# Decays of a selective scan: PSUM or SBUF for the units whose products GpSimd makes

## The chip, the core and the metric

The kernel runs on one core of a Trainium2 chip. A core has TensorE (PE, matrix multiplication), VectorE (DVE), ScalarE (ACT, activation functions) and GpSimd (POOL), each with its own instruction queue, and SyncE (SP), which here only issues transfers. Two memories on the core hold 128 partitions each: SBUF, and the smaller PSUM with eight banks, each of which holds 512 fp32 columns. The metric is device time in microseconds (us) for one execution.

## The reference

Four images of 64x64 positions and 128 channels go through four layers. Layer 0 holds the part that matters here, a selective scan in four directions over 4,096 positions, with 256 channels and 16 states for each channel:

```python
def step(h, t):
    x_t, d_t, B_t, C_t = t
    h = jnp.exp(d_t[..., None] * A) * h + (d_t * x_t)[..., None] * B_t[:, :, None, :]
    return (h, jnp.einsum('bkdn,bkn->bkd', h, C_t))
```

The factor `exp(d_t * A)` is the decay. Around the scan layer 0 has a projection, a depthwise 3x3 convolution, normalisations, a gate and an MLP. Layer 1 is attention over all positions of an image, layer 2 a chain of convolutions, layer 3 attention in 7x7 neighbourhoods with an MLP. Everything is fp32.

## The kernel before

**The scan unit.** `selective_scan` treats one image. It walks over the four directions, over eight chunks of 512 positions and over the states. One unit holds 32 channels with 4 states each on the 128 partitions, twice (g = 0, 1), and 512 columns. An image has 512 units, the kernel 2,048. A unit's steps are:

- POOL, L501: `dB` = `du` times a row of B, one instruction of 128x1024 for both g, all in SBUF. `dB` has four buffers.
- ACT, L507: for each g, the decay `dA` = exp(scale x `dt`), 128x512. All units share three PSUM tiles (`bufs=3`), each of one bank.
- DVE, L509: for each g, the scan over 512 columns, from `dA`, `dB` and the state that the chunk before left.
- ACT, L516 or L518: the last column is kept as the next chunk's state.
- The product of the scan's result with a row of C. `ON_POOL` says which engine makes it: in image 0 five, in the later images seven of 16 units have it made by POOL (L522, one instruction for both g). There the scan writes to the SBUF tile `hc`[...]. For the other units the scan writes back over the decay in PSUM and DVE makes the product into `hc` (L514, one instruction for each g).
- PE, L555: sums over the states into the PSUM tile `py`.

A unit is called a P unit below if POOL makes its product and a V unit if DVE does. DVE scans both kinds.

**What runs beside it.** `network` starts with `scan_inputs` for image 0, then scans image after image. Beside the scan of image 0 run `scan_inputs` for the other images; beside the scan of image n (n from 1 to 3) runs `rest` for image n-1, that is the output of its layer 0 (`scan_output`) and its layers 1 to 3; after the last scan, `rest` for image 3. Four of the eight PSUM banks belong to the scan (three for `dA`, one for `py`), the others to what runs beside it until the scan is over.

**Order.** The order on each engine is fixed when the program is built. A scheduler sets it from priorities and from its own idea of durations; the scan has lower priority than the layers beside it. On each engine the instructions then run strictly in that order, each waiting for semaphores of the others. `settle` puts POOL's product two units (`BEHIND`) after the scan that it needs.

**The product buffers.** Once image 0's scan is laid out and the inputs of all images are made, `network` opens an SBUF pool `ss_more` and hands it to `Products.widen`. From then on `products.more` is not None and four further `hc` buffers are in use; the pool lasts until the scan is over.

**Other lines that are named.** L396 and L397 (`softplus`): exp and log of 128x512 on ACT, the first from PSUM to PSUM, the second from PSUM to SBUF. L601 (`scan_output`): DVE adds two 128x128 SBUF tiles, once for each image. L785 (`layer1`): a DVE maximum over 4,096 columns of one SBUF tile. L854 (`layer1`, last image): DVE adds two SBUF tiles of 2,048 columns. L1165 (`layer3_bound`, once): a DVE instruction on one element with two SBUF inputs. L1390 (`layer3_attention`): DVE adds a PSUM tile to an SBUF tile, 512 columns.

Of the kernel before, what the change touches and what calls it, by code (L numbers as in the profile page):

```python
# [28 lines left out]
F32 = mybir.dt.float32  # L29
# [13 lines left out]
LC = 512  # L43
# [24 lines left out]
def mid(ap, n):  # L68

    return bc(ap.unsqueeze(1), [ap.shape[0], n, ap.shape[1]])  # L70
# [383 lines left out]
def selective_scan(tc, K, S, D, img):  # L454
# [9 lines left out]
    pool, psum, products = S.pool, S.psum, S.products  # L464
    waiting = []

    def settle(unit):
        while waiting and waiting[0][0] <= unit:
            waiting.pop(0)[1]()

    for k in ORDER:
# [4 lines left out]
        for i in range(NCH):  # L476
            c = NCH - 1 - i if back else i
            for hf in range(2):
# [11 lines left out]
                for j in range(NJS):  # L490
# [7 lines left out]
                    for pp in range(2):  # L498
                        pr = 2 * hf + pp
                        dB = pool.tile([128, 2, LC], F32, name="dB", bufs=4)  # L500
                        nc.gpsimd.tensor_mul(dB, dus[pp], mid(bt, 2))  # L501
                        on_pool = S.unit % 16 in ON_POOL[img > 0]
                        S.unit += 1
                        hc = products.tile()
                        for g in range(2):
                            dA = psum.tile([128, LC], F32, name="dA", bufs=3)
                            nc.scalar.activation(dA, dts[pp][:, g, :], AF.Exp, scale=S.A[:, k, j, pr, g : g + 1])  # L507
                            hg = hc[:, g, :] if on_pool else dA
                            nc.vector.tensor_tensor_scan(  # L509
                                hg[:, order], dA[:, order], dB[:, g, order],  # L510
                                0.0 if i == 0 else state[:, j, pr, g : g + 1], ALU.mult, ALU.add,
                            )
                            if not on_pool:
                                mm = nc.vector.tensor_mul(hc[:, g, :], dA, ct)  # L514
                                if i < NCH - 1:
                                    nc.scalar.copy(state[:, j, pr, g : g + 1], dA[:, last : last + 1])  # L516
                        if on_pool and i < NCH - 1:
                            nc.scalar.copy(state[:, j, pr, :], hc[:, :, last])  # L518
                        if on_pool:

                            def product(hc=hc, ct=ct, made=made):
                                made.append(nc.gpsimd.tensor_mul(hc, hc, mid(ct, 2)))  # L522

                            waiting.append((S.unit + BEHIND, product))
                        else:
                            made.append(mm)
                        hcs.append(hc)
                        settle(S.unit)
# [1151 lines left out]
def everything_again(tc, K, A, D, out):  # L1680

    K.general = True
    make_shifted_bias(tc, A, D.bias)
    for img in range(B):
        with ExitStack() as ctx:
            S = make_scan(ctx, tc, K, A)
            scan_inputs(tc, K, A, D, img)
            selective_scan(tc, K, S, D, img)
        with ExitStack() as ctx:
            xT = transposed(ctx, tc)  # L1690
            scan_output(tc, K, A, D, img, xT, None)
            layer1(tc, K, A, D, img, xT, False)
            layer2(tc, K, A, D, img, xT, False)
        layer3_shifted(tc, K, A, D, img)
        layer3_mlp_alone(tc, K, A, D, img, out[img], 4)


def network(tc, A, out):
    nc = tc.nc
    with ExitStack() as ctx:  # L1700
# [26 lines left out]
        with ExitStack() as scan_ctx:  # L1727
            S = make_scan(scan_ctx, tc, K, A)
            make_conv_diagonals(tc, K, A, D.conv_diag)
            with priority(tc, K, SCAN_FIRST // 2):  # L1730
                with tc.tile_pool(name="mk_w2", bufs=1, side="right") as pool:
                    make_layer2(tc, K, A, D, pool)
            scan_inputs(tc, K, A, D, 0)
            before = None
            for img in range(B):
                with priority(tc, K, SCAN_FIRST):
                    selective_scan(tc, K, S, D, img)
                if img == 0:
                    make_bias(tc, K, A, D.biasT)
                    for later in range(1, B):  # L1740
                        scan_inputs(tc, K, A, D, later)
                    more = scan_ctx.enter_context(tc.tile_pool(name="ss_more", bufs=1))
                    S.products.widen(more, 4)
                else:
                    rest(tc, K, A, D, img - 1, before)
                    before = img - 1, out[img - 1]
            rest(tc, K, A, D, B - 1, before, scan_ctx.close, out[B - 1])
# [84 lines left out]
```

## Time and profile before

| | |
|---|---|
| median of 3 runs | 8,847.33 us (8,841.02 to 8,850.56) |
| the profiled execution | 8,838.78 us |
| its span, first to last instruction | 8,837.0 us |
| mean TensorE clock granted | 0.860 |
| busy: PE, DVE, ACT, POOL | 7,047.0, 7,137.4, 5,686.9, 7,046.7 us |
| scan of image 0 | 103 to 2,165 us |
| scan of images 1, 2, 3 | 2,165 to 3,983, to 5,815, to 7,637 us |
| after the scan | 7,637 to 8,837 us |

The profile is of one execution. Its page has the busy time of each engine, the span in 40 slices (a digit is the busy share in tenths), the DMA queues, and groups of instructions by line, engine, operation and tile: out<-in, shape and count, then busy us and mean ns of one, then the idle time of the engine before them and what ended most of it. The trace answers further views: sums of each engine's busy time in chosen stretches; waits (engine, line, tile, what it waited for, then total us, times, longest); one line's durations (shortest/median/longest); and a timeline, where a row gives start, length in us, engine, line, operation, tiles and how many instructions of a kind follow each other (x2 means that the length is of both). Idle time of an engine that doesn't set the end costs nothing.

### The profile page before, as it was taken

The page shows a single profiled execution, that of the slowest core. Times are in us where ns is not written, and L with a number is a line of the kernel's source. Part 1 is how long each engine was busy: PE and PEld are TensorE (multiplying, and loading weights), DVE is VectorE, ACT ScalarE, POOL GpSimd, SP SyncE. Part 2 cuts the span into 40 slices and gives each one's busy share as a digit, 9 for nine tenths or more (in the row PEclk, how much of TensorE's full clock was granted, in tenths as well). Part 3 has the DMA queues.
Part 4 walks back from the last instruction along what each step waited for, and adds up shares of the span by engine and source line. Part 5 has one row for each costly group of instructions (what it writes and reads, how often), then busy time and mean ns, then how long its engine had stood idle before and what let it go on. Part 6 is the DMA issues. An engine that isn't in the chain of part 4 may idle for free. (4 is left out here: it accounts for less than half of the span.)

```text
span 8837.0 us, 102218 instructions
## 1 busy us (share of the span) xinstructions
PE 7047.0 (80%) x30532; PEld 2635.0 (30%) x30532; DVE 7137.4 (81%) x8531; ACT 5686.9 (64%) x11661; POOL 7046.7 (80%) x3079
## 2 busy tenths in 40 slices
PE   6745858687788898786788988877789887788988
PEld 2211313132332222333322223333322223344333
DVE  4788978787999999998899999998899999513433
ACT  5646767676676676666766676667766666454366
POOL 6888998989899999997799999998899989500000
PEclk8756869697799998898899998888899998899989
DMA  5777777777554556665455556575455565320020
GB/s 185 244 232 247 241 251 240 260 242 262 189 170 165 170 170 219 191 211 190 160 168 173 174 174 227 194 224 176 156 171 174 176 217 192 108 70 5 1 82 12
DMA packets 855474, 1572.03 MB, mean 178 GB/s; under 512 B 218341, under 2 KB 336764, under 8 KB 851197
## 3 DMA queue, kind: packets, MB, share of 16 engines
q1 hardware_dynamic: 724605, 1389.21, 48.1%
q10 hardware_dynamic: 130304, 176.19, 5.6%
q8 instruction: 245, 4.01, 0.2%
q14 instruction: 320, 2.62, 0.1%
HBM read 1273.92 MB, written 280.18 MB: 176 GB/s over the span
## 5 line engine op out<-in xcount | busy, mean ns | idle before, releaser
L501 POOL TENSOR_TENSOR dB<-du,b_rows 128x1024 f32<-128x1024 f32 x2048 | 4805.9, 2375 | 477.2 <-issue 124.7
L507 ACT ACTIVATE dA<-dt,w_A_log 128x512 f32<-128x512 f32 x4096 | 2781.9, 690 | 510.8 <-DVE hc L509 246.7
L509 DVE TENSOR_TENSOR_SCAN dA<-dA,state,dB 128x512 f32<-128x512 f32 x2128 | 2631.5, 1272 | 275.6 <-POOL dB L501 131.8
L522 POOL TENSOR_TENSOR hc<-hc,c_rows 128x1024 f32<-128x1024 f32 x832 | 1976.6, 2376 | 47.0 <-ACT state L518 21.7
L509 DVE TENSOR_TENSOR_SCAN hc<-dA,state,dB 128x512 f32<-128x512 f32 x1456 | 1801.1, 1267 | 180.5 <-ACT dA L507 105.8
L514 DVE TENSOR_TENSOR hc<-dA,c_rows 128x512 f32<-128x512 f32 x2432 | 1564.5, 675 | 74.4 <-PE py L555 59.3
L555 PE MATMUL py<-hc,pick 128*32 128x512 f32 x8192 | 1245.1, 683 | 392.0 <-POOL hc L522 299.8
L516 ACT COPY state<-dA 128x1 f32<-128x1 f32 x2128 | 326.9, 158 | 1271.7 <-DVE hc L514 1260.1
L845 PE MATMUL pa<-e,l_v 128*128 128x512 f32 x2048 | 1062.5, 651 | 20.3 <-ACT e L801 20.3
L797 PE MATMUL pair<-l_g,l_f 32*128 32x512 f32 x2048 | 532.8, 667 | 165.7 <-ACT e L801 119.1
L801 ACT ACTIVATE e<-pair 128x1024 f32<-128x1024 f32 (+1 forms) x448 | 508.4, 1135 | 231.4 <-PE pair L797 222.8
L985 POOL MEMSET l_h<- 64x128 f32 x8 | 1.6, 197 | 814.9 <-DVE l_h L959 814.9
L845 PEld LDWEIGHTS pa<-e,l_v 128*128 128x128 f32 x2048 | 374.3, 199 | 670.9 <-issue 615.1
L555 PEld LDWEIGHTS py<-hc,pick 128*32 128x32 f32 x8192 | 210.1, 116 | 1161.4 <-issue 471.1
L247 PE MATMUL ps<-band,w_conv_diag 128*128 128x504 f32 (+3 forms) x1152 | 500.4, 594 | 6.0 <-ACT delta L397 6.0
L1351 PE MATMUL pair<-table,ident 128*128 128x512 f32 x768 | 408.2, 657 | 98.7 <-ACT e L1361 76.2
L509 DVE TENSOR_TENSOR_SCAN dA<-dA,dB 128x512 f32<-128x512 f32 x304 | 356.1, 1212 | 66.3 <-POOL dB L501 52.5
L201 PE MATMUL ps<-ident,ln_xn 128*128 128x128 f32 x512 | 141.9, 371 | 325.2 <-ACT ln_xn L198 253.2
L328 POOL TENSOR_TENSOR du<-delta,xc 128x1024 f32<-128x1024 f32 x128 | 333.3, 2611 | 52.6 <-ACT delta L397 46.7
L1361 ACT ACTIVATE e<-pair 128x1024 f32<-128x1024 f32 (+1 forms) x224 | 254.8, 1137 | 178.6 <-PE pair L1355 177.8
L247 PEld LDWEIGHTS ps<-band,w_conv_diag 128*128 128x128 f32 x1152 | 221.3, 193 | 283.9 <-issue 263.8
L797 PEld LDWEIGHTS pair<-l_g,l_f 32*128 32x128 f32 x2048 | 140.6, 189 | 523.9 <-ACT e L801 264.4
(285 smaller groups left out, 8746.8 us busy)
## 6 DMA issues: line engine op xcount, KB each, us to landing
b_rows<-bc_dram SPq DMA_DIRECT2D x1024, 256.0 KB
c_rows<-bc_dram SPq DMA_DIRECT2D x1024, 256.0 KB
dt<-delta_dram SPq DMA_DIRECT2D x512, 512.0 KB
du<-du_dram SPq DMA_DIRECT2D x512, 512.0 KB
delta_dram<-delta ACTq DMA_DIRECT2D x128, 512.0 KB
du_dram<-du SPq DMA_DIRECT2D x128, 512.0 KB
table<-biasT_dram SPq DMA_DIRECT2D x72, 512.0 KB
y_first_dram<-y_sum ACTq DMA_DIRECT2D x128, 256.0 KB
```

What stands on the lines that cost most here:

```text
L247: mm = nc.tensor.matmul(out[:, r0 - row0 : r1 - row0, c0:c1], lhsT((dy + 1) * 3 + dx + 1), src[:, r0 + dy : r1 + dy, c0 + dx : c1 + dx], s ...
L328: nc.gpsimd.tensor_mul(du.rearrange("p d (a b) -> p d a b", b=H), deltas[b].rearrange("p d (a b) -> p d a b", b=H), tk,)
L501: nc.gpsimd.tensor_mul(dB, dus[pp], mid(bt, 2))
L507: nc.scalar.activation(dA, dts[pp][:, g, :], AF.Exp, scale=S.A[:, k, j, pr, g : g + 1])
L509: nc.vector.tensor_tensor_scan(hg[:, order], dA[:, order], dB[:, g, order], 0.0 if i == 0 else state[:, j, pr, g : g + 1], ALU.mult, ALU.add,)
L514: mm = nc.vector.tensor_mul(hc[:, g, :], dA, ct)
L522: made.append(nc.gpsimd.tensor_mul(hc, hc, mid(ct, 2)))
L555: mm = nc.tensor.matmul(py[0][32 * q : 32 * q + 32, :], S.pick, hcs[q // 2][:, q % 2, :], start=(k == 1 and j == 0), stop=(j == NJS - 1),)
L797: nc.tensor.matmul(ps[:, u, :], f[quad, t // 4, span(t % 4, 128)], g[quad, c, :], start=True, stop=True)
L801: made = nc.scalar.activation(e, ps, AF.Exp)
L845: nc.tensor.matmul(pa, v[:, 8 * q + t, :], es[q], start=(t == 0 and q == 0), stop=(t == 7 and q == 3),)
L1351: nc.tensor.matmul(ps[:, u, :], K.ident, t[:, u, :], start=True, stop=False)
```

## The change

Where a unit is a P unit and `products.more` exists, which is so from image 1 on, the decay is a tile of the SBUF pool `ss_more`, named `decays`, with three buffers of 128x512. In all other cases it is the PSUM tile `dA` as before. So in images 1 to 3 the three PSUM tiles hold decays of V units only, and the P units' scans read both the decay and `dB` from SBUF. Instructions, shapes and counts are the same.

```diff
                         hc = products.tile()
                         for g in range(2):
-                            dA = psum.tile([128, LC], F32, name="dA", bufs=3)
+                            if on_pool and products.more is not None:
+                                dA = products.more.tile([128, LC], F32, name="decays", bufs=3)
+                            else:
+                                dA = psum.tile([128, LC], F32, name="dA", bufs=3)
                             nc.scalar.activation(dA, dts[pp][:, g, :], AF.Exp, scale=S.A[:, k, j, pr, g : g + 1])
                             hg = hc[:, g, :] if on_pool else dA
                             nc.vector.tensor_tensor_scan(
```

## The prediction

> **What bounds the kernel now.** I read the 40 slices of the page first, to cut the span into stages; then the sums by stage; then the costliest groups, the waits of VectorE (DVE), and the timelines of DVE and GpSimd (POOL) where a DVE instruction was oddly long.
>
> ```profile
> DVE  4788978787999999998899999998899999513433
> POOL 6888998989899999997799999998899989500000
> ```
>
> Both are at 80 to 100% until slice 35 and POOL then stops: the scan fills nearly all of the span. By the starts of the scan instructions, image 0 is scanned from 103 to 2165 us and images 1 to 3, which alone the edit touches, from 2165 to 7637 us, 5,472 us in all. The sums of these three stages:
>
> ```profile
> core 0: us, PE busy (x) PEld busy (x) DVE busy (x) ACT busy (x) POOL busy (x), PEclk, DMA share, GB/s
> 2165.00:3983.00 1818.00, 1505.29 (x7009) 542.65 (x7012) 1688.75 (x1942) 1197.46 (x2451) 1730.48 (x750) 0.88 0.58 188
> 3983.00:5815.00 1832.00, 1517.16 (x6823) 556.91 (x6818) 1678.62 (x1984) 1242.31 (x2564) 1705.87 (x740) 0.88 0.56 183
> 5815.00:7637.00 1822.00, 1512.80 (x6840) 556.71 (x6839) 1678.85 (x1978) 1240.55 (x2551) 1707.42 (x740) 0.89 0.56 182
> ```
>
> POOL is busy 5,144 of 5,472 us (94%, idle 328), DVE 5,046 (92%, idle 426), ScalarE (ACT) 3,680 (67%). The two lean on each other all the time. The price of each step stands in the groups of the page:
>
> ```profile
> L501 POOL TENSOR_TENSOR dB<-du,b_rows 128x1024 f32<-128x1024 f32 x2048 | 4805.9, 2375 | 477.2 <-issue 124.7
> L507 ACT ACTIVATE dA<-dt,w_A_log 128x512 f32<-128x512 f32 x4096 | 2781.9, 690 | 510.8 <-DVE hc L509 246.7
> L522 POOL TENSOR_TENSOR hc<-hc,c_rows 128x1024 f32<-128x1024 f32 x832 | 1976.6, 2376 | 47.0 <-ACT state L518 21.7
> L509 DVE TENSOR_TENSOR_SCAN hc<-dA,state,dB 128x512 f32<-128x512 f32 x1456 | 1801.1, 1267 | 180.5 <-ACT dA L507 105.8
> L514 DVE TENSOR_TENSOR hc<-dA,c_rows 128x512 f32<-128x512 f32 x2432 | 1564.5, 675 | 74.4 <-PE py L555 59.3
> ```
>
> The scans that write hc are those of GpSimd's units ("P units"), whose product is L522; VectorE's own ("V units") have theirs in L514. What more PSUM tiles could win is in DVE's waits within 2165 to 7637 us:
>
> ```profile
> DVE hc L509 <- ACT dA L507: 96.3, 56, 7.0
> DVE dA L509 <- POOL dB L501: 81.0, 91, 5.1
> DVE dA L509 <- ACT dA L507: 60.6, 41, 4.6
> ```
>
> Waits for a decay come to 157 us. No gain from the added depth can be larger, and behind it stand the waits for dB (122 us with those of the hc scans).
>
> [...] Today each scan reads dA in PSUM and dB in SBUF, one SBUF input, and no scan row shows a block (1,267 ns). After the edit the P units' scans read two. Does the trace know the block? Yes, at L601, an add of two 128x128 SBUF tiles. First DVE's timeline, then POOL's, at that place (start, length):
>
> ```profile
> 2217.06 11.22 DVE L601 TENSOR_TENSOR center<-center,ident 128x128 f32<-128x128 f32 x1
> 2228.20 2.32 DVE L509 TENSOR_TENSOR_SCAN hc<-dA,dB 128x512 f32<-128x512 f32 x2
> ```
>
> ```profile
> 2216.60 6.93 POOL L501 TENSOR_TENSOR dB<-du,b_rows 128x1024 f32<-128x1024 f32 x3
> 2223.50 2.33 POOL L522 TENSOR_TENSOR hc<-hc,c_rows 128x1024 f32<-128x1024 f32 x1
> 2225.79 2.33 POOL L501 TENSOR_TENSOR dB<-du,b_rows 128x1024 f32<-128x1024 f32 x1
> 2230.66 2.44 POOL L501 TENSOR_TENSOR dB<-du,b_rows 128x1024 f32<-128x1024 f32 x1 [2.54 <-DVE hc L509]
> ```
>
> The add takes 0.29 us where POOL is silent (its last occurrence, at 7776 us); here it lasts 11.22 us, through five POOL instructions, and ends 0.16 us after the fifth. Another took 5.60 us, at 5902 us. L1165, a SCALAR_TENSOR_TENSOR of one element with two SBUF inputs, took 5.05 us amid POOL's work, and ended at an edge between two POOL instructions. The control:
>
> ```profile
> L785 DVE TENSOR_REDUCE bounds<-l_v x4: 4412/4420/4420, 2539.4 to 8046.8; 128x1 f32<-128x4096 f32 x4
> ```
>
> A one-input reduction of 4,096 columns has the same length under POOL's work and after it. [...] no row shows a scan with two SBUF inputs, nor POOL held behind DVE.
>
> [...] L854, both inputs in SBUF, takes 2,293 ns for 2,048 columns[...], and L1390, one input in PSUM, 677 ns for 512[...]. I take 0 for it[...]. [...] here L397 (to SBUF) takes 601 ns, L396 (to PSUM) 580.
>
> **The change part by part.** In images 1 to 3, 7 of 16 units are P units: 3 x 512 x 7/16 = 672 units, each with two decays and two scans, so 1,344 of each. No instruction and no DMA is added or removed; in the rebuilt order side work stands 3 to 10 scans later in the mean, 40 at most, of 4,096. I cost that at nothing.
>
> (a) ACT writes 1,344 decays to SBUF: 1,344 x 21 ns = 28 us on an engine idle a third of the time. Nothing on the path; were that cover gone, 28 us.
>
> (b) The three PSUM tiles serve V units alone: a gain of 0 to 157 us, if nothing else came. It can't show while DVE stands longer in (c): 0.
>
> (c) 1,344 scans get a second SBUF input. Two scans of one unit last 2.45 us (timeline of the steady state). While they run, POOL's dB and products, all of which read SBUF, are shut out; while POOL runs, the scans are. So POOL's work and these scans add up: 672 x 2.45 = 1,646 us on top of 5,144 gives 6,790 us if POOL is never idle otherwise, and 7,118 us if it keeps its 328 us of idle time. I take the second, since those gaps come from side work, transfers and full buffers that stay: **+1,646 us**; the low end is 6,790 - 5,472 = +1,318.
>
> Does DVE bear that? A P unit followed by a V unit: POOL has two dB and one product, 7.1 us. DVE has 2.45 (P), then 2.45 + 1.26 (V) and 0.6 of side work, 4.3 us in which POOL may work. 7.1 - 4.3 = 2.8 us of POOL's work falls where DVE stands before its P scans. The pair takes 2.45 + 7.1 = 9.6 us, against 7.1 to 7.3 now. Over the stage: 7,118 - 5,046 = 2,072 us of DVE not working, less 304 of today's other waits, is 2.6 us for each P unit, 1.3 per scan.
>
> (d) New waits. Behind a scan that stands, in DVE's order, are V scans, their products and the statistics of other layers; ACT's copies of state wait for them, and with them later decays, since ACT's order is fixed too. A decays tile is free only when the scan three earlier ended. POOL may run four dB ahead (bufs=4), then stops for want of a free one; that is where DVE gets in at the latest, so nothing locks up and POOL's run ahead is not lost.
>
> Sum against the profiled execution: 8,838.8 + 1,646 = 10,485 us. The median of the three runs is 8.5 us above that execution: 10,493, rounded to 10,500.
>
> **The rivals.** *Every scan yields.* [...] the first scan waits half a POOL instruction and the second a whole one (2.35 us): 672 x 3.53 = 2,372 us, 5,046 + 304 + 2,372 = 7,722, that is +2,250 and 11,100 us; with a whole one for each, 11,880. L601, passed over four times, speaks for it; that POOL stops when its four buffers are full speaks against it.
> *POOL is not held.* Only DVE waits, half to a whole instruction per P unit: 672 x 1.18 to 2.35 = 790 to 1,580 us, so 9,640 to 10,430. In favour: no row shows POOL held. [...]
> *The scan takes no lock (the other side).* If a scan[...] reads its second input some other way, (c) is 0 and (b) is left, about half of 157 us since the waits for dB come next: 8,770 us, faster. It decides if the P scans still last under 1.3 us. Against it: L1165 shows that an instruction of that family with two SBUF inputs waits.
> That the edit does nothing can be left out: the rebuilt program has 1,344 decays in SBUF, and as many scans that read them.
>
> **How the numbers follow.** The lock as in (c): 0.62, 10,165 to 10,800. Every scan yields: 0.20. POOL is not held: 0.10. No lock: 0.08. The range 10,000 to 11,400 leaves out the last, half of the third and the top of the second, 0.18 together. Within 0.2%, some 18 us, is about what a measurement of this kernel can't tell from no change; only a no-lock case with a tiny gain lands there, 0.02. Faster 0.06, slower 0.92.
>
> **What would show it.** Right: P scans (hc from decays) at a mean of 2.3 to 3 us with V scans still at 1.27; images 1 to 3 taking some 2,370 us each while image 0 and the last 1,200 us keep their lengths; POOL's dB rows longer or with gaps of 1.3 to 2.5 us ended by DVE; DVE's waits for decays no longer in front. Wrong: P scans at 1.27 us, or a stage of images 1 to 3 under 1,900 us.

## The result, and the profile after

The changed kernel takes 10,219.9 us (10,217.7 to 10,222.0 in five runs), the kernel before 8,843.9 us beside it: a ratio of 1.1555, with a 95% interval of 1.1540 to 1.1571. The prediction was 10,500 us with a range of 10,000 to 11,400, and slower with a chance of 0.92. The profiled execution has a span of 10,220.2 us.

The slices of the page after, DVE and POOL as before:

```profile
DVE  5798887879999999999999999999999999922433
POOL 6988989887888888887888878887788888810000
```

DVE has become full from the second image on, and POOL has gone from nines to eights. The starts of the scans put images 1 to 3 at 2,178 to 8,989 us, 6,811 us in all against 5,472. Image 0 takes 2,074 us (2,062 before) and the time after the scan 1,231 us (1,200), so 1,339 of the 1,383 us between the two profiled spans lie where the edit acts. The sums of the three stages, with the columns of the view before:

```profile
2178.00:4462.00 2284.00, 1656.13 (x7012) 588.75 (x7012) 2226.97 (x1942) 1214.28 (x2452) 1905.48 (x751) 0.81 0.45 149
4462.00:6727.00 2265.00, 1646.65 (x6731) 592.52 (x6723) 2221.44 (x1977) 1250.80 (x2546) 1872.68 (x741) 0.81 0.45 148
6727.00:8989.00 2262.00, 1678.64 (x6815) 601.75 (x6811) 2224.70 (x1975) 1252.72 (x2547) 1872.42 (x737) 0.81 0.45 147
```

DVE: busy 6,673 us (5,046 before), idle 138 (426). POOL: busy 5,651 us (5,144), idle 1,160 (328). The same work is done, so the 1,627 us by which DVE's busy time grew are waits inside instructions: an instruction that waits after its start has a longer row, and the whole row counts as busy (2,506 ns in the groups below for a scan that takes 1,267 elsewhere). The granted TensorE clock in these stages fell from 0.88 to 0.81, but this isn't the cause: PE stands idle longer than before (1,829 us, 937 before), and DVE waits for PE 36 us in all (42 before). What lowered the clock was not tried. The groups say which instructions wait (lines stand three lower than before):

```profile
L501 POOL TENSOR_TENSOR dB<-du,b_rows 128x1024 f32<-128x1024 f32 x2048 | 5267.2, 2581 | 1215.2 <-issue 368.8
L512 DVE TENSOR_TENSOR_SCAN hc<-decays,state,dB 128x512 f32<-128x512 f32 x1176 | 2902.1, 2506 | 7.3 <-PE py L558 7.3
L512 DVE TENSOR_TENSOR_SCAN dA<-dA,state,dB 128x512 f32<-128x512 f32 x2128 | 2619.8, 1267 | 151.3 <-ACT dA L510 75.3
L525 POOL TENSOR_TENSOR hc<-hc,c_rows 128x1024 f32<-128x1024 f32 x832 | 1992.6, 2395 | 144.4 <-issue 82.7
L510 ACT ACTIVATE dA<-dt,w_A_log 128x512 f32<-128x512 f32 x2752 | 1870.5, 691 | 317.0 <-DVE hc L517 198.4
L517 DVE TENSOR_TENSOR hc<-dA,c_rows 128x512 f32<-128x512 f32 x2432 | 1559.3, 673 | 76.6 <-PE py L558 63.1
L510 ACT ACTIVATE decays<-dt,w_A_log 128x512 f32<-128x512 f32 x1344 | 965.7, 719 | 699.7 <-DVE hc L512 678.5
```

The scans that read their decay from SBUF last 2,506 ns in the mean, twice the 1,267 of those that read it from PSUM; the V units' products are as before (673 ns, 675 before). ACT's decays take 28 ns more in SBUF than in PSUM. POOL's dB rows have grown by 206 ns over the whole kernel. In DVE's waits within 2,178 to 8,989 us, what led the list before has nearly gone:

```profile
DVE dA L512 <- ACT dA L510: 18.6, 18, 3.5
DVE dA L512 <- POOL dB L501: 12.6, 2, 9.4
```

How the two engines take turns is seen in a timeline of each, at the same place; a row with x2 or x3 joins instructions of one kind:

```profile
4998.01 5.63 DVE L512 TENSOR_TENSOR_SCAN hc<-decays,state,dB 128x512 f32<-128x512 f32 x2
5003.56 2.44 DVE L512 TENSOR_TENSOR_SCAN dA<-dA,state,dB 128x512 f32<-128x512 f32 x2
5005.91 1.26 DVE L517 TENSOR_TENSOR hc<-dA,c_rows 128x512 f32<-128x512 f32 x2
```

```profile
4996.98 5.57 POOL L501 TENSOR_TENSOR dB<-du,b_rows 128x1024 f32<-128x1024 f32 x2
5003.77 2.35 POOL L525 TENSOR_TENSOR hc<-hc,c_rows 128x1024 f32<-128x1024 f32 x1 [1.22 <-issue]
5006.08 7.98 POOL L501 TENSOR_TENSOR dB<-du,b_rows 128x1024 f32<-128x1024 f32 x3
```

The two scans of a P unit take 5.63 us here, and two of a V unit 2.44. POOL's two dB take 5.57 us, 0.87 more than twice 2.35. The second of them alone:

```profile
4999.29 3.26 POOL L501 TENSOR_TENSOR dB<-du,b_rows 128x1024 f32<-128x1024 f32 x1
```

The first scan waited for the first dB to end (4,999.33 us) and ended 1.08 us later, at 5,000.41. The second dB was held meanwhile: its row is 0.91 us longer than 2.35. The second scan then waited for that dB to end (5,002.55 us) and ended 1.09 us later. So the waiting goes both ways.

POOL's next instruction comes after a gap of 1.22 us, 0.13 us after the scan. The view names no semaphore for it ("issue"), yet it needn't be the scan's hold on POOL: this L525 is the product of the very unit whose scan had just ended, and needs its result. Paired in this way over the whole stage (products with the scans of their own units, each dB with the scan that frees its buffer, four units earlier), 719 of POOL's 750 gaps over 0.1 us, 1,070 of 1,156 us, end within 0.3 us after the scan that the instruction needs. Whether the scan would have held these instructions without that need can't be told from the trace. What the scans took from POOL shows in the rows: 487 of 1,534 dB and 34 of 672 products last over 2.7 us, the dB rows among them 3.29 us in the mean. Before the change none did.

### The profile page after: what moved, and what is told of

Its sections match the earlier page's. It is cut to its first block, busy times and chain, and to the rows that moved or that the text cites. A ratio compares the mean times of both kernels' runs of the same rounds, so it can differ in the third digit from the quotient of the medians.

```text
span 10220.2 us, 101831 instructions
## 1 busy us (share of the span) xinstructions
PE 7509.3 (73%) x30532; PEld 2767.1 (27%) x30532; DVE 8767.7 (86%) x8531; ACT 5736.5 (56%) x11661; POOL 7557.3 (74%) x3079
## 5 line engine op out<-in xcount | busy, mean ns | idle before, releaser
L501 POOL TENSOR_TENSOR dB<-du,b_rows 128x1024 f32<-128x1024 f32 x2048 | 5267.2, 2581 | 1215.2 <-issue 368.8
L512 DVE TENSOR_TENSOR_SCAN hc<-decays,state,dB 128x512 f32<-128x512 f32 x1176 | 2902.1, 2506 | 7.3 <-PE py L558 7.3
L512 DVE TENSOR_TENSOR_SCAN dA<-dA,state,dB 128x512 f32<-128x512 f32 x2128 | 2619.8, 1267 | 151.3 <-ACT dA L510 75.3
L525 POOL TENSOR_TENSOR hc<-hc,c_rows 128x1024 f32<-128x1024 f32 x832 | 1992.6, 2395 | 144.4 <-issue 82.7
L510 ACT ACTIVATE dA<-dt,w_A_log 128x512 f32<-128x512 f32 x2752 | 1870.5, 691 | 317.0 <-DVE hc L517 198.4
L510 ACT ACTIVATE decays<-dt,w_A_log 128x512 f32<-128x512 f32 x1344 | 965.7, 719 | 699.7 <-DVE hc L512 678.5
L848 PE MATMUL pa<-e,l_v 128*128 128x512 f32 x2048 | 1198.0, 722 | 72.0 <-ACT e L804 70.9
L521 ACT COPY state<-hc 128x2 f32<-128x2 f32 x728 | 140.1, 193 | 965.9 <-DVE hc L512 958.3
L1354 PE MATMUL pair<-table,ident 128*128 128x512 f32 x768 | 471.0, 745 | 277.5 <-ACT e L1364 217.1
L804 ACT ACTIVATE e<-pair 128x1024 f32<-128x1024 f32 (+1 forms) x448 | 507.6, 1133 | 211.0 <-PE pair L800 201.9
L512 DVE TENSOR_TENSOR_SCAN hc<-decays,dB 128x512 f32<-128x512 f32 x168 | 402.5, 2433 | 0.0
L512 DVE TENSOR_TENSOR_SCAN hc<-dA,state,dB 128x512 f32<-128x512 f32 x280 | 348.6, 1267 | 61.3 <-ACT dA L510 33.4
```

The source lines that it names most:

```text
L512: nc.vector.tensor_tensor_scan(hg[:, order], dA[:, order], dB[:, g, order], 0.0 if i == 0 else state[:, j, pr, g : g + 1], ALU.mult, ALU.add,)
L804: made = nc.scalar.activation(e, ps, AF.Exp)
L848: nc.tensor.matmul(pa, v[:, 8 * q + t, :], es[q], start=(t == 0 and q == 0), stop=(t == 7 and q == 3),)
L1354: nc.tensor.matmul(ps[:, u, :], K.ident, t[:, u, :], start=True, stop=False)
```

## The experiments

The theory: a scan with two SBUF inputs and POOL's instructions shut each other out. The rivals: three decay tiles are too few; writing the decays to SBUF, or the new order, is the cost; only DVE waits, and POOL isn't held. Stage lengths below are for images 1 to 3, from the starts of the scans.

**More tiles.** Five decay tiles in place of three:

```diff
-                                dA = products.more.tile([128, LC], F32, name="decays", bufs=3)
+                                dA = products.more.tile([128, LC], F32, name="decays", bufs=5)
...
-                    S.products.widen(more, 4)
+                    S.products.widen(more, 3)
```

> The changed kernel with five SBUF tiles for decays in place of three (one of the four extra hc buffers is given up for the room). Theory (the two-input scans and POOL's instructions shut each other out, and their times add up): depth changes nothing, 10,150 to 10,280 us, P scans still at a mean of 2.4 to 2.5 us. Rival (three tiles are too few: ACT stands 678 us before decays until a scan has freed a tile, and DVE gets its decays late): well below, by 200 us or more, and P scans nearer 1.27 us.

Measured: 10,155.9 us, ratio 1.1483 (1.1462 to 1.1504), within the theory's range. One of the four further `hc` buffers was given up for the room. P scans have a mean of 2,473 and 2,572 ns (with and without a state from the chunk before), and ACT still stands 653 us before decays. The stage took 6,787 us, so in it five tiles are worth 24 us, under a fiftieth of the loss. Most of the other 40 us lie after the scan (1,193 us in place of 1,231), where no decay is made; that part isn't explained.

**The second SBUF input taken away.** The P units' scans read a constant PSUM tile; ACT's writes to SBUF stay:

```diff
+        S.fixed = psum.tile([128, LC], F32, name="fixed", bufs=1)
+        nc.vector.memset(S.fixed, 0.5)
...
-                                dA = psum.tile([128, LC], F32, name="dA", bufs=3)
+                                dA = psum.tile([128, LC], F32, name="dA", bufs=2)
...
-                                hg[:, order], dA[:, order], dB[:, g, order],
+                                hg[:, order], src[:, order], dB[:, g, order],
```

Here `src` is the constant for P units from image 1 on.

> The changed kernel, but the P units' scans of images 1 to 3 read a constant PSUM tile in the place of their decay; ACT still writes the decays to SBUF and each scan still waits for its own. The constant takes one bank, so the V units have two PSUM tiles in place of three. The scan's decay values are thus left out of the P units. Theory (the second SBUF input is the cost): P scans return to 1.27 us and POOL's dB to 2.38 us; 8,750 to 9,000 us. Rival (writing the decays to SBUF, or the changed order on ACT and DVE, is the cost): 9,600 us or more.

Measured: 9,240.5 us, ratio 1.0443 (1.0427 to 1.0459), between the two expectations. The groups decide it:

```profile
L517 DVE TENSOR_TENSOR_SCAN hc<-fixed,state,dB 128x512 f32<-128x512 f32 x1176 | 1439.0, 1264 | 3.4 <-POOL dB L504 2.2 <-PE py L565 1.1
L504 POOL TENSOR_TENSOR dB<-du,b_rows 128x1024 f32<-128x1024 f32 x2048 | 4803.0, 2362 | 891.2 <-DVE dA L517 341.8 <-DVE hc L517 180.9 <-issue 142.0
```

With one SBUF input the P scans are back at 1,264 ns and POOL's dB at 2,362, although the decays are still written to SBUF. That kernel's other loss is not in the instructions but in waits of V units for decays, and image 0, where there is no P unit's constant at work, took 2,268 us. The missing PSUM tile was suspected; hence the control.

**The control: two PSUM tiles in the kernel before.** The edit is `bufs=2` for `dA`.

> The kernel before with two PSUM tiles for decays in place of three, for all units. A control for the kernel with the constant PSUM tile, whose image 0 ran in the same way and took 2,268 us. Theory (what that kernel lost, 393 us, is the price of its missing PSUM tile): image 0 at 2,268 us again, images 1 to 3 at 1,950 to 2,050 us each, since here P units share the two tiles; the whole 9,300 to 9,650 us. Rival (the constant tile's kernel lost its time elsewhere): image 0 near 2,062 us, the whole under 9,100 us.

Measured: 9,155.2 us, ratio 1.035 (1.032 to 1.038), under the theory's 9,300 to 9,650 us and over the rival's 9,100. Image 0 took 2,263 us, as expected, and images 1 to 3 took 5,733 us together, 1,911 each, less than I had priced. The kernel with the constant took 5,719 us for them. So the missing tile accounts for that kernel's loss in these stages. That kernel's whole is 85 us longer all the same: after the scan it took 1,157 us and this control 1,050, where neither edit acts, and this stays open. The pair also says something on the aim of the change: with two PSUM tiles, taking the P units out of PSUM altogether gave 14 us of 5,733 in these stages. These are one profile each, and the runs of the constant's kernel lie up to 23 us apart, so no gain is shown.

**Half of the scans.** Only the first decay of a P unit goes to SBUF:

```diff
-                            if on_pool and products.more is not None:
+                            if on_pool and g == 0 and products.more is not None:
```

> Only the first of a P unit's two decays goes to SBUF, so 672 scans have two SBUF inputs in place of 1,344. Theory (the times add up, POOL has no idle left): images 1 to 3 take 5,144 + 672 x 1.225 = 5,967 us, the whole 9,340 us; up to 9,450 if some of POOL's idle time stays. Rival (each such scan costs DVE the same wait, whatever POOL does): half of the loss, 9,530 us. Rival (POOL isn't held, DVE waits 0.93 us for the first scan of a unit): 672 x 0.93 less what DVE's idle time takes up, 9,150 to 9,250 us.

Measured: 9,463.7 us, ratio 1.0704 (1.0688 to 1.0720); the stage took 6,065 us. None of the three numbers is met exactly: it is 14 us over the theory's upper end, 66 under the linear rival, and 214 over the rival in which POOL isn't held, which falls. Two groups stand side by side in this kernel:

```profile
L512 DVE TENSOR_TENSOR_SCAN hc<-decays,state,dB 128x512 f32<-128x512 f32 x588 | 1501.9, 2554 | 2.5 <-PE py L558 2.5
L512 DVE TENSOR_TENSOR_SCAN hc<-dA,state,dB 128x512 f32<-128x512 f32 x868 | 1084.9, 1257 | 63.0 <-ACT dA L510 40.1 <-POOL dB L501 12.7 <-issue 4.3
```

Same line, same kind of unit, same engine: 2,554 ns with the decay in SBUF, 1,257 with it in PSUM (588 of the second row are the other scans of the same units, 280 are of image 0). In DVE's account the loss is the added wait less the idle time that it takes up: 830 - 237 = 593 us for 672 scans, 1,627 - 288 = 1,339 us for 1,344. The wait per scan is the same (1.2 us), and the idle time can be used only once; so in this account half of the scans cost 0.44 of the loss. POOL's account shows its side directly: with the same work, its rows in these stages grew from 5,144 to 5,659 us, 515 of the 593 us.

**DVE's share alone.** The kernel before with one tiny DVE instruction ahead of each P unit's scan, `made_dA` being the decay's ACTIVATE:

```diff
+                                spot = pool.tile([128, 1], F32, name="spot", bufs=4)
+                                tiny = nc.vector.tensor_mul(spot, dB[:, g, 0:1], dB[:, g, 1:2])
+                                after(tc, tiny, made_dA)
```

> The kernel before (all decays in PSUM) with one tiny DVE instruction ahead of each P unit's scan in images 1 to 3, 1,344 in all: the product of two single columns of dB, so two SBUF inputs. Nothing of the output uses it. [...] this shows DVE's share of the lock without POOL's. Theory (DVE must wait for POOL's current instruction to end, some 1 us at a random moment, each time): the tiny rows at a mean of 0.9 to 1.4 us, 9,600 to 10,300 us, POOL's dB rows unchanged at 2.36 to 2.40 us. Rival (only POOL being shut out costs anything; DVE's waits hide in its idle time): no more than 100 us over the kernel with the one-SBUF-input instruction.

And with one SBUF input, the first operand being `dA[:, 0:1]` in PSUM:

> The same as the kernel with the tiny two-SBUF-input instruction, in the same order, but the tiny instruction multiplies a column of the PSUM decay with a column of dB: one SBUF input. Theory: the rows take about 0.15 us, 1,344 x 0.15 = 200 us of DVE, of which its idle time takes up a part: 8,900 to 9,100 us. Rival (the added instructions and their semaphores, not the second SBUF input, make the other kernel slow): as slow as that one.

Measured: 9,830.4 us, ratio 1.1115 (1.1083 to 1.1147), and 8,928.9 us, ratio 1.0095 (1.0066 to 1.0125), both as the theory had it. The tiny rows, and POOL's dB of the first of the two kernels:

```profile
L512 DVE TENSOR_TENSOR spot<-dB 128x1 f32<-128x1 f32 x1344 | 1242.0, 937 | 88.2 <-ACT dA L507 84.5 <-ACT state L523 2.7
```

```profile
L512 DVE TENSOR_TENSOR spot<-dA,dB 128x1 f32<-128x1 f32 x1344 | 193.4, 148 | 183.0 <-ACT dA L507 174.0 <-ACT state L523 4.0 <-POOL dB L501 1.2
```

```profile
L501 POOL TENSOR_TENSOR dB<-du,b_rows 128x1024 f32<-128x1024 f32 x2048 | 4805.6, 2355 | 1362.9 <-DVE hc L514 381.6 <-issue 364.4 <-DMA c_rows<-bc_dram 89.5
```

One column takes 148 ns with one SBUF input and 937 ns with two, in the same place. POOL's dB isn't lengthened (2,355 ns, 2,375 in the kernel before) by an instruction whose shortest row is 96 ns. The stages differ by 6,460 - 5,570 = 890 us. That is DVE's waiting for POOL alone; the changed kernel lost 1,339 us with as many two-input instructions. The other some 450 us I put down to POOL being held by full-length scans; that split is an inference from two kernels, not one measurement. POOL's rows fit it: over images 1 to 3 they grew by 10 us here and by 507 us in the changed kernel.

**All units.** The edit carried to V units too, by dropping `on_pool` from the condition:

> The edit carried to all units of images 1 to 3: V units' decays lie in the three SBUF tiles too, so 3,072 scans and 1,728 of DVE's products have two SBUF inputs. Theory (POOL's instructions and DVE's two-SBUF-input instructions shut each other out, and their times add up to a floor): 5,144 + 3,072 x 1.225 + 1,728 x 0.64 = 10,013 us for images 1 to 3, the whole 13,390 us, 13,200 to 13,800. Rival (each such instruction makes DVE wait the 1.24 us that it waits in the changed kernel): 5,046 + 4,800 x 1.24 + 140 = 11,140 us, the whole 14,510 us. Rival (the loss comes from P and V units keeping their decays in different memories, and the order that follows): no more than the changed kernel's 10,220 us.

Measured: 12,944.5 us, ratio 1.4633 (1.4591 to 1.4676). The loss grows with the number of two-input instructions, which ends the rival of mixed memories. It is below both other numbers and below the theory's range; the theory's came 3% too high. V units' products now suffer too, while P scans hardly wait:

```profile
L517 DVE TENSOR_TENSOR hc<-decays,c_rows 128x512 f32<-128x512 f32 x1728 | 3866.0, 2270 | 3.5
L512 DVE TENSOR_TENSOR_SCAN decays<-decays,state,dB 128x512 f32<-128x512 f32 x1512 | 3134.8, 2107 | 19.2 <-POOL dB L501 11.1 <-ACT decays L510 7.9
L512 DVE TENSOR_TENSOR_SCAN hc<-decays,state,dB 128x512 f32<-128x512 f32 x1176 | 1612.6, 1404 | 17.9 <-ACT decays L510 11.1 <-POOL dB L501 6.8
```

The product takes 2,270 ns in place of 675, and a P scan 1,404. Two SBUF inputs alone don't make an instruction wait; it also takes a POOL instruction that is at work just then. In the trace that was so at the start of 119 of the 1,344 P scans: these last 2.82 us in the mean, all others 1.25. DVE's rows grew by 4,378 us over 4,800 instructions, 0.91 us each in the mean. The stage took 9,500 us where the sum gave 10,013: 513 us over 4,800 instructions, 0.11 us each. So the sum isn't a strict floor: the two engines overlap by at least that much at a hand-over. The changed kernel shows the same: 1,037 of its P scans were kept waiting over 0.3 us by a POOL instruction, and they ended 1.08 us after it, where a scan alone lasts 1.26. So 0.18 us of the scan overlaps the instruction that it waits for.

**A version that uses the SBUF otherwise.** Decays in PSUM as before, with a fifth dB buffer from image 1 on in 4 of the 6 KB:

```diff
-                        dB = pool.tile([128, 2, LC], F32, name="dB", bufs=4)
+                        S.turn = getattr(S, "turn", 0) + 1
+                        if products.more is not None and S.turn % 5 == 0:
+                            dB = products.more.tile([128, 2, LC], F32, name="dB", bufs=1)
+                        else:
+                            dB = pool.tile([128, 2, LC], F32, name="dB", bufs=4)
```

> The kernel before with a fifth dB buffer from image 1 on (4 KB of the SBUF that the decays took), decays in PSUM for all. Theory (with one SBUF input per scan, what is left are the waits of DVE for dB, 122 us, and of POOL for a free dB, 75 us, while DVE and POOL take turns in being late): 8,740 to 8,830 us. Rival (the waits for decays, 157 us, take over whatever dB gives): within 0.2% of the kernel before.

Measured: 8,829.9 us against 8,846.8, ratio 0.9981 (0.9975 to 0.9988). It beats both kernels, by a fifth of a per cent; 17 us fits the end of the theory's range and the rival alike. Its profiled execution, 8,838.4 us, was no faster than the one before, and in it images 1 to 3 took 5,467 us (5,472 before), so this profile doesn't show where the 17 us come from. That stays open. More dB buffers in the changed kernel, where POOL's gaps end with a dB buffer that comes free, weren't tried.

## Why the prediction was right

**Step (c), the lock: right in kind, 307 us too dear.** That POOL and these scans shut each other out (the lock), so that their times add up, was my estimate. The rows after show both kept waiting: P scans at 2,506 ns where 1,267 is usual, and 487 of 1,534 dB at 3.29 us where 2.36 is. The prediction had 5,144 + 1,646 us and then added POOL's 328 us of idle time as staying. The stage took 6,811 us, against 6,790 for the sum without idle time and 7,118 with it. Take the last 1.22 us of each P scan's row in the trace as its work. Then 260 us of the stage have neither a POOL row nor a P scan at work, so most of the idle time stayed, as foretold. The term that was mis-sized is the price of the scans to POOL: 903 us outside POOL's rows and 507 us by which the rows grew, 1,410 us in place of 1,646. The prediction let a scan begin when POOL's instruction has ended; the trace has 0.18 us of overlap, some 240 us over 1,344 scans. That the sum without idle time is met within 21 us is luck: it leaves out the idle time and the overlap, which are nearly equal.

**The wait per scan: right.** Foretold were 1.3 us per scan and P scans at 2.3 to 3 us; they came to 2,506 ns with a state and 2,433 without, 1.24 us of wait in the mean. V scans stayed at 1,267 ns. Images 1 to 3 took 2,284, 2,265 and 2,262 us, 4% under the 2,370 foretold.

**Who goes when: the first rival's picture, not its price.** I argued that POOL goes on until its dB buffers are full and that both scans of a unit then run together. The trace shows them split: scan, one POOL instruction, scan. In the mean over the 672 units the first scan lasts 2.20 us and the second 2.79, waits of 0.9 and 1.5 us where that rival had 1.18 and 2.35. It asked for 11,100 us and falls by its size. POOL's stop for want of a free dB does come, but at the second scan: 637 dB of the stage start after a gap and within 0.3 us of the scan that freed their buffer, 131 before the change. So the foretold wait per scan came out right though the order behind it was only half right.

**POOL is held.** The rival without it gave 9,640 to 10,430 us, so the total alone doesn't refute it. The longer dB rows do (2,581 against 2,375 ns over the whole kernel), with the 515 of 593 us in the kernel with half of the scans, and the 450 us between the tiny two-input instruction and the full scan fit. POOL's gaps decide nothing, since nearly all end with a scan that POOL needed anyway.

**The scan takes no lock: refuted** by the P scans' length (2,506 ns), and by the same scan at 1,257 and 2,554 ns in one kernel.

**Step (a), 28 us on ACT, hidden: within 24 us.** A decay took 28 ns more in SBUF (estimated 21). What I missed is the depth of three, but it is small: ACT stood 678 us before decays, and five tiles shortened the stage by 24 us.

**Step (b), 0 to 157 us, set at 0: borne out.** DVE's waits for dA fell from 157 to 19 us, and the total shows no gain from it: DVE stands elsewhere. Whether the PSUM tiles or merely DVE's own lateness ended those waits isn't told apart. At two PSUM tiles the same relief without the lock gave 14 us, less than the runs of one kernel differ. With three it wasn't tried, since the constant tile would come on top of the eight banks that the scan and the layers beside it hold, and stays open.

**PSUM against SBUF as a source, 0 taken.** The prediction gave a DVE instruction no gain and no loss from reading SBUF in place of PSUM. The shortest P scan with a state is 1,246 ns, the shortest V scan 1,169 and the median V scan 1,261, so these rows show no gain from SBUF as the source.

**A reading too round, and without effect.** The slices of DVE and POOL that I read as 80 to 100% busy up to slice 35 hold a 4, a 6 and several sevens. The sums by stage, on which the prediction rests, are read rightly.

## What to carry to other kernels

Before moving a DVE operand from PSUM to SBUF, count the SBUF inputs that its instructions then have and look at what GpSimd does at that time: beside a GpSimd that is nearly always at work, a scan with two SBUF inputs waited 1.24 us in the mean here and a product of one column 0.79, and the scans held GpSimd in return (a mean dB of 2,581 ns, 2,375 before). Where GpSimd stood idle, as at most P scans of the kernel with all units changed, there was no wait to speak of (1.25 us for a scan). One odd row in the profile before, an add of 0.29 us that lasted 11.22, was the sign of a loss of 15%; rows with a mean far above their shape are worth a timeline of both engines.

## What the runs showed of the hardware

- A scan (TENSOR_TENSOR_SCAN) with both inputs in SBUF shuts out GpSimd's multiplications and is shut out by them, as an add is (0.29 us alone, 11.22 beside GpSimd): 2,506 ns against 1,267 for the scan, and 487 of 1,534 of GpSimd's multiplications at 3.29 us where 2.36 is usual.
- A scan cost GpSimd less than its own length: 0.93 us in those rows, where the scan alone lasts 1.26. A scan that was kept waiting ends 1.08 us after GpSimd's instruction, so 0.18 us of it overlaps.
- An instruction of one column on VectorE waits too: 937 ns with two SBUF inputs, 148 with one, in the same place.
- GpSimd's blocked time shows as a longer row when it has started: 3.26 us for the dB at 4,999.29 us, where 2.35 is usual. A gap is no proof: 719 of 750 gaps here ended with a scan that the next instruction needed, though the view names that scan for a part of them only.
- As a rule the two engines took turns after one instruction on each side: 1,141 of 1,344 P scans have the end of one GpSimd instruction within their row, 6 of more than one. Yet L601, before the change, was passed over at four edges between GpSimd's instructions in its row of 11.22 us. What decides that was not tried.
